# Latent attention: causal masks added by 64-row instead of 32-row matmuls, and a new order of units and of other work on TensorE

## The chip, the cores and the metric

The kernel runs on one core of a Trainium2 chip. The metric is device time in microseconds for one execution of the whole program, as a median of runs.

## What is computed

The reference is a "macaron" block over x of shape 8 x 512 x 128 (batch, tokens, channels): a local-attention transformer at half weight, a latent attention, and the same transformer again.

```python
x = x + 0.5 * _L0_ffn_ref(_layernorm(x), ...)
x = x + _L0_attn_ref(_layernorm(x), ...)
x = x + 0.5 * _L0_ffn_ref(_layernorm(x), ...)
```

The change touches the middle line alone:

```python
k_eff = (W_dq.T @ W_uq.T @ W_uk).reshape(nh, hs, n_kvl)
v_eff = jnp.transpose((W_uv.T @ W_o.T).reshape(n_kvl, nh, hs), (1, 0, 2))
c_kv = x @ W_dkv.T
q = (x @ W_dq.T @ W_uq.T).reshape(B, T, nh, hs)
q_lat = jnp.einsum('bqhd,hdl->bhql', q, k_eff)
attn = jnp.einsum('bhql,bkl->bhqk', q_lat, c_kv) / sqrt(hs)
attn = jnp.where(causal[None, None], attn, -jnp.inf)
attn = jax.nn.softmax(attn, axis=-1)
y_lat = jnp.einsum('bhqk,bkl->bhql', attn, c_kv)
y = jnp.einsum('bhql,hld->bqhd', y_lat, v_eff).reshape(B, T, C)
```

There are 16 heads of 8 channels, 512 tokens, and a causal mask.

## The kernel before

The program has three parts: the first transformer (`ffn("f0")`), `latent_attention`, and the second transformer (`ffn("f1")`). The two transformers are ordered by a planner with costs and places; the latent attention is ordered by hand, in the loop at the end of `latent_attention`, and `in_order` keeps every TensorE (PE) instruction in the order in which the program makes it.

**Layout.** The product of the weights is folded, so that a head's scores are a product over its 8 channels plus one more row. Heads lie in quadrants of 32 rows: head 4g + j has its channels in rows 32g to 32g + 8 of `q_heads` and `k_heads`, at index j. Row 32g + 8 (`MD::32`) holds the negated maximum on the query side and ones on the key side, so that the second pass over the scores comes out already shifted. Three sets of heads (`NSETS`) are used by turns over the 8 batches. A product over 32 rows occupies one quadrant of PE's rows (`32*128` in the profile), so that four can run side by side; the f32 products are made in two passes, which the trace shows as two matmuls with a weight load each. PSUM has seven banks of 512 columns for such products (`unit_bank`) and one for the values (`lo`).

**Two passes per batch.** `maxima_steps` (tile `sc`, lines L1038 and L1045) computes the scores with queries on partitions and reduces their maxima on DVE (L1051, L1053); its `finish` transposes them and sends them by a DMA into the heads. `sum_steps` (tile `st`, lines L1100 and L1107) computes the transposed scores, with keys on partitions; ACT takes the exponentials into `pl` (L1114). Both have ten steps a batch. A step has four units, one per quadrant g, and a unit fills one bank: one or two blocks of scores, 512 columns in all. The lists `MAXIMA` and `SUMS` say which blocks a unit holds; a unit has one or two blocks on the diagonal, which have to be masked.

**Masks.** The mask is added in PSUM by bf16 matmuls ahead of the f32 products: `rows_of` picks rows, and `causal` or `causal_t` holds the mask for them. A unit makes four such matmuls, each for 32 rows of the mask and in the unit's own quadrant (`quadrant(g)`). GpSimd (POOL) builds the three masks at the start of this part (L1205, L1213).

**Values.** `multiply` (L1123) multiplies the exponentials of a block by the values, for the four quadrants side by side in columns (`128*32`), into the bank `lo`; when a head group j has its four blocks, ACT copies the bank to `os` (L1132), and `update` transposes it (L1146), divides it by the sums (L1151, L1153) and adds it to X on POOL (L1157).

**The order.** Batch b's sums run beside the maxima of batch b + 1, which are two steps (`LEAD`) ahead. A step is made in two halves: `run_together([units[g], other[g]])` for g = 0 and 1, then for g = 2 and 3. `run_together` takes one matmul from each unit by turns. The maxima units are turned by two quadrants (`(g + 2) % 4`), so that the two units of a pair lie in different quadrants. Behind the first half come the products with the values of the step before (`held`). Behind the second half comes other work: a piece of the projections of batch b + 2 (`latent_project_steps`: normalisation, transposes, q, k, values, one piece a step from step 0 on), or a finished head group's `update`. The first batch's maxima run alone at the start; in the last two steps of the second-last batch and in the last batch there are no more maxima to run, and the sums run alone, two units at a time.

Of the kernel before, what the change touches and what calls it, by code (L numbers as in the profile page):

```python
# [9 lines left out]
BF16 = mybir.dt.bfloat16  # L10
AF = mybir.ActivationFunctionType
ALU = mybir.AluOpType
# [3 lines left out]
P = 128  # L16
MASKED = -1.0e30
# [172 lines left out]
def kernel(  # L190
# [22 lines left out]
    B, T, C = x.shape  # L213
# [17 lines left out]
    wk, lw, lp, lc = (PartPool() for _ in range(4))  # L231
# [88 lines left out]
    for first in (True, False):  # L320
        band = const.tile([P, 4, P], BF16, name=f"band{int(first)}")
        nc.gpsimd.memset(band, 0.0)
        for half in (0, WIN):
            rows = band[half : half + WIN]
# [14 lines left out]
    for l in range(L):  # L339
        t = const.tile([P, 4, NB, DH], F32, name=f"tab{l}")  # L340
        for s in range(2):
            g = qk_sc[:, l, s]
# [614 lines left out]
    def in_order(ins):  # L957
        return tc.keep_in_program_order(ins)
# [3 lines left out]
    def heads_of(b):  # L962
        return q_heads[b % NSETS], k_heads[b % NSETS], v_heads[b % NSETS]
# [49 lines left out]
    def quadrant(g):  # L1013
        return slice(32 * g, 32 * g + 32)


    MAXIMA = (
        [[((3, j), 0)] for j in range(4)]
# [4 lines left out]
    def maxima_steps(b):  # L1023


        qp, kp, _ = heads_of(b)
        nm = sm.tile([P, 4, 4, NB], F32, tag="lnm", name=f"lnm_{b}")

        nb = sm.tile([P, 4, 4, NB], F32, tag="lnb", name=f"lnb_{b}")

        def unit(held, g):
            rows = quadrant(g)
            (i0, j0), _ = held[0]
            bank = unit_bank(f"sc_{b}_{i0}_{j0}_{g}")
            blocks = bank.rearrange("p (n w) -> p n w", w=P)
            diag = {3: blocks[:, 3:], 2: blocks[:, 2:], 1: blocks[:, 1::2]}[i0]
            for k in range(4):
                yield lambda k=k: nc.tensor.matmul(  # L1038
                    diag[:, :, 32 * k :], lhsT=masks["rows_of"][rows, k],
                    rhs=masks["causal"][rows, k, 32 * k :].unsqueeze(1)  # L1040
                    .to_broadcast([32, len(held), P - 32 * k]),
                    start=(k == 0), stop=False, skip_group_check=True,
                )
            for n, ((i, j), at) in enumerate(held):
                yield lambda i=i, j=j, at=at, n=n: nc.tensor.matmul(  # L1045
                    bank[:, at : at + (i + 1) * P], lhsT=qp[rows, j, i * P : (i + 1) * P],
                    rhs=kp[rows, j, : (i + 1) * P],
                    start=False, stop=(n == len(held) - 1), skip_group_check=True,
                )
            if i0 == 2:  # L1050
                nc.vector.tensor_reduce(nb[:, g, j0], blocks, AX.X, ALU.max, negate=True)  # L1051
            else:
                nc.vector.tensor_reduce(  # L1053
                    nm[:, g, j0 : j0 + len(held), i0],
                    bank.rearrange("p (u w) -> p u w", u=len(held)), AX.X, ALU.max, negate=True,
                )

        def finish():
            nc.vector.tensor_reduce(nm[:, :, :, 2], nb[:, :, :, 0:3], AX.X, ALU.min)
            nc.vector.tensor_copy(nm[:, :, :, 0], nb[:, :, :, 3])  # L1060
            tp = unit_bank(f"tp_nm_{b}")
            in_order(nc.tensor.transpose(
                tp[: 16 * NB, :P], nm.rearrange("p g j n -> p (g j n)"), ident
            ))
            nT = lw.tile([16 * NB, P], F32, tag="lnT", name=f"lnT_{b}")
            nc.vector.tensor_copy(nT, tp[: 16 * NB, :P])
            nc.sync.dma_start(out=qp[MD::32], in_=nT)

        return [[unit(held, (g + 2) % 4) for g in range(4)] for held in MAXIMA], finish


# [13 lines left out]
    def sum_steps(b):  # L1085
# [5 lines left out]
        def unit(held, g, res):  # L1091
            rows = quadrant(g)
            (c0, j0), _ = held[0]
            bank = unit_bank(f"st_{b}_{j0}_{c0}_{g}")

            blocks = bank.rearrange("p (n w) -> p n w", w=P)
            diag = {0: blocks[:, :1], 1: blocks[:, ::3], 2: blocks[:, ::2]}[c0]
            for k in range(4):
                cut = 32 * k + 32
                yield lambda k=k, cut=cut: nc.tensor.matmul(  # L1100
                    diag[:, :, :cut], lhsT=masks["rows_of"][rows, k],
                    rhs=masks["causal_t"][rows, k, :cut].unsqueeze(1)
                    .to_broadcast([32, len(held), cut]),
                    start=(k == 0), stop=False, skip_group_check=True,
                )
            for n, ((c, j), at) in enumerate(held):
                yield lambda c=c, j=j, at=at, n=n: nc.tensor.matmul(  # L1107
                    bank[:, at : at + T - c * P],
                    lhsT=kp[rows, j, c * P : (c + 1) * P], rhs=qp[rows, j, c * P :],
                    start=False, stop=(n == len(held) - 1), skip_group_check=True,  # L1110
                )
            pr = lp.tile([P, 512], F32, tag="pl", name=f"pl_{b}_{j0}_{c0}_{g}")
            with exponentials():
                nc.scalar.activation(pr, bank, AF.Exp, scale=MSCALE)  # L1114
            res[g] = pr
# [19 lines left out]
        def values(held, res):  # L1135


            todo = kept + [(c, j, at, res) for (c, j), at in held if j == held[0][0][1]]
            kept[:] = [(c, j, at, res) for (c, j), at in held if j != held[0][0][1]]
            rest = [multiply(*what) for what in todo]  # L1140
            return next((r for r in rest if r is not None), None)

        def update(j, os_):
            tp = unit_bank(f"tp_o_{b}_{j}")
# [22 lines left out]

    def run_together(units):

        units = [u for u in units if u is not None]  # L1170
        while units:
            for u in list(units):
                ins = next(u, None)
                if ins is None:
                    units.remove(u)
                else:
                    in_order(ins())


    q_heads, k_heads, v_heads = [], [], []  # L1180
    masks = {}

    def latent_attention():
        no_shift = lc.tile([4, T], F32, tag="no_shift", name="no_shift")
# [16 lines left out]


        for name in ("rows_of", "causal", "causal_t"):
            masks[name] = lc.tile([P, 4, P], BF16, tag=name, name=name)
            nc.gpsimd.memset(masks[name], 0.0)  # L1205
        for g in range(4):
            for name, pattern, sign, op, fill in (
                ("rows_of", [[-32, 4], [1, P]], -1, ALU.not_equal, 1.0),
                ("causal", [[32, 4], [-1, P]], 1, ALU.is_ge, MASKED),
                ("causal_t", [[-32, 4], [1, P]], -1, ALU.is_ge, MASKED),  # L1210
            ):
                rows = masks[name][quadrant(g)]
                nc.gpsimd.affine_select(  # L1213
                    out=rows, in_=rows, pattern=pattern, compare_op=op, fill=fill, base=0,
                    channel_multiplier=sign,
                )
        for k in range(1, NSETS):
            blank(k, nc.gpsimd)
        full = latent_weights()
# [9 lines left out]
            maxima.append(steps)  # L1229
        assert len(maxima[0]) == NS  # L1230
        for step in maxima[0]:
            run_together(step[:2])
            run_together(step[2:])
        ahead = [step for steps in maxima[1:] for step in steps]
        after = []
        finish[0]()
        for _ in range(LEAD):
            step = ahead.pop(0)
            run_together(step[:2])
            run_together(step[2:])  # L1240
        held = None
        projecting = None
        for b in range(B):
            for s, (units, values) in enumerate(sum_steps(b)):
                other = ahead.pop(0) if ahead else None
                if s == 0 and b + 2 < B:
                    projecting = latent_project_steps(b + 2, full, no_shift)
                for half in (0, 2):
                    if other is not None:
                        for g in (half, half + 1):  # L1250
                            run_together([units[g], other[g]])
                    else:
                        run_together(units[half : half + 2])
                    if half == 0 and held is not None:
                        rest = held()
                        if rest is not None:
                            after.append(rest)
                held = values
                if s == NS - LEAD and b + 1 < B:
                    finish[b + 1]()  # L1260
                if projecting is not None and next(projecting, "end") == "end":
                    projecting = None
                if projecting is None and after:
                    after.pop(0)()
                elif len(after) > 1:
                    after.pop(0)()
        after.append(held())
        for rest in after:
            rest()

    with part(WORK_F, s=1, mm=1):
        ffn("f0", last=False)
# [89 lines left out]
```

## Time and profile before

| what | us |
|---|---|
| median of 3 runs (1949.81 to 1952.99) | 1952.13 |
| the profiled execution | 1953.01 |
| its span, first to last instruction | 1950.9 |
| from 792.8 to 829.8: the first batch's maxima and the two steps ahead | 37.0 |
| from 829.8 to 1153.2: sums and maxima side by side, 68 steps | 323.4 |
| from 1153.2 to 1200.5: sums alone, 12 steps | 47.3 |
| L1045 and L1107, f32 score products, 2 x 1024 matmuls (busy time) | 227.5 and 212.8 |
| L1114, exponentials, 320 of 597 ns (busy time) | 176.2 |

The profile is of one execution. Its groups give a line, an engine, an operation, the tiles and the shape with a count and a mean; `32*128` ahead of a shape is the part of PE's array, rows times columns, that a matmul uses. A matmul's start is recorded and its end is modelled; matmuls in different parts of the array overlap, so that busy times of groups add up to more than the stretch that they lie in. What a stretch costs is read from the distances of starts in the timeline. The granted TensorE clock is 0.984 of full speed as a mean.

### The profile page before, as it was taken

The numbers are of one execution on the slowest core, as the hardware profiler recorded it, in microseconds if no ns is written. First come the engines' busy times: TensorE is split into PE (matmuls) and PEld (weight loads), VectorE is DVE, ScalarE is ACT, GpSimd is POOL, SyncE is SP. The second block draws the span as 40 slices with busy tenths as digits, with TensorE's granted clock in tenths as the row PEclk, the third lists the DMA queues.
The fourth block names the chain that finished last, engine by engine and source line by source line (L and its number), as shares of the span: only waits on it lengthen the run. The fifth ranks groups of instructions, "written<-read, shape, count | busy, mean of one in ns | idle before, by whom it ended". The sixth has DMA issues, their size and how long they took to land.

```text
span 1950.9 us, 51021 instructions
## 1 busy us (share of the span) xinstructions
PE 1799.2 (92%) x19860; PEld 1186.0 (61%) x19860; DVE 1381.3 (71%) x2896; ACT 1394.7 (71%) x3921; POOL 985.4 (51%) x1673
## 2 busy tenths in 40 slices
PE   2889999999999997799999998889999999999998
PEld 1556666666666665566666663566666666666665
DVE  4888887777777775766655543887787777777764
ACT  1888888888888883155555554778888888888785
POOL 3876666666666653100000001867666666666651
PEclk9999999999999998799999998999999999999999
DMA  4111111111111110000000000111111011111110
GB/s 129 28 35 23 23 23 26 23 29 24 27 24 31 23 23 8 26 14 15 14 14 14 14 2 1 26 28 29 26 23 23 23 26 23 34 30 33 28 36 23
DMA packets 51729, 50.05 MB, mean 26 GB/s; under 512 B 23302, under 2 KB 34288, under 8 KB 51488
## 3 DMA queue, kind: packets, MB, share of 16 engines
q1 hardware_dynamic: 47132, 42.58, 9.3%
q10 hardware_dynamic: 4356, 4.20, 0.7%
q8 instruction: 158, 2.59, 0.6%
q14 instruction: 83, 0.68, 0.1%
HBM read 6.30 MB, written 2.10 MB: 4 GB/s over the span
## 4 chain that ended last, share of the span: by engine, by line
PE 56%; DVE 23%; ACT 11%; issue 5%; POOL 3%; DMA 1%; SPq 0%; ACTq 0%; DVEq 0%; POOLq 0%
PE mm_f L535 8%; PE mm_f L504 7%; PE mm_f L836 6%; ACT pr_f L679 5%; PE st L1107 5%; DVE c_f L545 5%; DVE s_f L548 4%; PE lo L1123 4%; PE mm_f L878 4%; PE sc L1045 4%; PE mm_f L745 4%; PE mm_f L769 4%; ACT sq_f L558 3%; PE sc_f L662 3%; PE st L1100 2%
## 5 line engine op out<-in xcount | busy, mean ns | idle before, releaser
L679 ACT ACTIVATE pr_f<-sc_f,nm_f,q_f 128x128 f32<-128x128 f32 x1024 | 460.2, 474 | 4.5 <-DVE nm_f L672 4.1
L535 PE MATMUL mm_f<-wqkv,hT_f 128*128 128x512 f32 x768 | 395.1, 616 | 35.7 <-DVE s_f L548 11.8
L564 POOL TENSOR_TENSOR qk_f<-c_f,s_f 128x512 f32<-128x512 f32 x256 | 324.5, 1271 | 109.8 <-DVE s_f L548 94.1
L687 POOL TENSOR_TENSOR pr_f<-pr_f,rso_f 128x512 f32<-128x512 f32 x256 | 265.8, 1039 | 215.2 <-DVE rso_f L703 142.1
L1114 ACT ACTIVATE pl<-st 128x512 f32<-128x512 f32 x320 | 176.2, 597 | 183.2 <-PE st L1107 111.8
L545 DVE TENSOR_TENSOR c_f<-mm_f,tab 128x512 f32<-128x512 f32 x256 | 175.2, 684 | 88.7 <-ACT sq_f L558 36.0
L558 ACT ACTIVATE sq_f<-mm_f 128x512 f32<-128x512 f32 x256 | 152.9, 603 | 115.1 <-DVE s_f L548 65.4
L1045 PE MATMUL sc<-k_heads,q_heads 32*128 32x384 f32 (+3 forms) x1024 | 227.5, 469 | 4.8 <-DMA k_heads<-kl 4.8
L679 ACT ACTIVATION_READ_ACCUMULATOR pr_f<-sc_f,nm_f,q_f 128x1 f32 x1024 | 225.1, 220 | 0.0
L1157 POOL TENSOR_TENSOR X<-X,lon 128x128 f32<-128x128 f32 x32 | 14.4, 452 | 402.6 <-DVE lon L1153 365.2
L1107 PE MATMUL st<-q_heads,k_heads 32*128 32x384 f32 (+3 forms) x1024 | 212.8, 435 | 0.0
L836 PE MATMUL mm_f<-fT_f,w 128*128 128x512 f32 (+1 forms) x384 | 189.9, 609 | 2.4 <-ACT fT_f L824 1.7
L504 PEld LDWEIGHTS mm_f<-ident,qk_f 128*128 128x128 f32 x1024 | 114.4, 142 | 125.1 <-POOL qk_f L600 50.2
L535 PEld LDWEIGHTS mm_f<-wqkv,hT_f 128*128 128x128 f32 x768 | 124.2, 192 | 100.8 <-issue 50.9
L745 PEld LDWEIGHTS mm_f<-pT_f,V_f 128*64 128x64 f32 (+1 forms) x4096 | 147.4, 136 | 55.3 <-issue 14.9
L671 DVE TENSOR_REDUCE nm_f<-sc_f 128x8 f32<-128x1024 f32 x128 | 154.7, 1209 | 36.9 <-PE sc_f L662 36.5
L745 PE MATMUL mm_f<-pT_f,V_f 128*64 128x64 f32 (+1 forms) x4096 | 179.8, 230 | 0.9 <-ACT pT_f L725 0.9
L504 PE MATMUL mm_f<-ident,qk_f 128*128 128x128 f32 x1024 | 161.6, 282 | 20.1 <-ACT kT_f L630 5.8
L548 DVE TENSOR_TENSOR s_f<-mm_f,tab 128x512 f32<-128x512 f32 x256 | 173.7, 678 | 0.0
L1053 DVE TENSOR_REDUCE lnm<-sc 128x1 f32<-128x512 f32 (+1 forms) x192 | 122.2, 685 | 71.6 <-PE sc L1045 49.7
L504 PE MATMUL mm_f<-ident,pr_f 128*128 128x128 f32 x1024 | 153.1, 278 | 11.8 <-ACT kT_f L630 6.2
L504 PEld LDWEIGHTS mm_f<-ident,pr_f 128*128 128x128 f32 x1024 | 117.4, 141 | 66.7 <-issue 39.8
(145 smaller groups left out, 3715.1 us busy)
## 6 DMA issues: line engine op xcount, KB each, us to landing
V_f<-V_f SPq DMA_DIRECT2D x224, 128.0 KB
hs_f<-Y SPq DMA_DIRECT2D x32, 112.0 KB
X<-in_x_dram SPq DMA_DIRECT2D x8, 256.0 KB
q_heads<-ql SPq DMA_DIRECT2D x64, 32.0 KB
k_heads<-kl SPq DMA_DIRECT2D x64, 32.0 KB
out_dram<-hs_f SPq DMA_DIRECT2D x8, 256.0 KB
wqkv<-in_wqkv_dram ACTq DMA_DIRECT2D x2, 768.0 KB
w<-in_w_dram ACTq DMA_DIRECT2D x2, 341.0 KB
```

The costliest lines, as they stand in the source:

```text
L504: nc.tensor.transpose(dst[:, i * P : (i + 1) * P], src(i), ident)
L535: nc.tensor.matmul(ps.tile, lhsT=hT[:, i * P : (i + 1) * P], rhs=wqkv_sb[l][:, at * INNER : (at + 1) * INNER], start=True, stop=True,)
L545: nc.vector.tensor_mul(c1.tile, psv, tabs[l][:, 2 * s, i].unsqueeze(1).to_broadcast([P, H, DH]))
L548: nc.vector.tensor_mul(s1.tile.rearrange("p h (t d) -> p h t d", t=2), psv.rearrange("p h (t d) -> p h t d", t=2)[:, :, ::-1], tabs[l][:, ...
L558: lambda s=s, ps=ps: nc.scalar.activation(sq[:, s], ps.tile, AF.Square),
L564: lambda s=s, c1=c1, s1=s1: nc.gpsimd.tensor_add(qk[:, s].rearrange("p (h d) -> p h d", d=DH), c1.tile, s1.tile),
L679: nc.scalar.activation(pr[:, h], sv[:, h % 2, h // 2], AF.Exp, bias=nm[:, h % 2, h // 2 : h // 2 + 1], scale=q8[:, h : h + 1], accum_out=s ...
L687: nc.gpsimd.tensor_mul(pr[:, heads], pr[:, heads], inv[:, heads].unsqueeze(2).to_broadcast([P, H // 2, P]),)
L745: nc.tensor.matmul(o[r * DH : (r + 1) * DH, u * P + w * WIN : u * P + (w + 1) * WIN], lhsT=(V2, V)[w][keys, i, h * DH : (h + 1) * DH], rhs ...
L836: nc.tensor.matmul(ps[: hsz[c], :], lhsT=w1_sb[l][:, at + c * P : at + c * P + hsz[c]], rhs=fT.tile, start=True, stop=True,)
L1045: yield lambda i=i, j=j, at=at, n=n: nc.tensor.matmul(bank[:, at : at + (i + 1) * P], lhsT=qp[rows, j, i * P : (i + 1) * P], rhs=kp[rows, ...
L1107: yield lambda c=c, j=j, at=at, n=n: nc.tensor.matmul(bank[:, at : at + T - c * P], lhsT=kp[rows, j, c * P : (c + 1) * P], rhs=qp[rows, j, ...
```

## The change

Masks are added by two matmuls of 64 rows in place of four of 32, in the half of the rows in which the unit's quadrant lies (`half_of`). `rows_of`, `causal` and `causal_t` have two blocks in place of four, and six selections build them in place of twelve.

`run_together` takes up to three units by turns and the fourth one behind them. It is called with all four units of a half step (sums, maxima, sums, maxima), with the four units of a step of the first batch's maxima, and with the four units of a step where sums run alone; the products with the values then come behind all four.

`values` returns its products one by one. In steps without a projection, a finished update or lone sums, the last product is made behind the second half. The projection pieces come in steps 1, 2, 4 and 6 (the normalisation ahead of step 0), and updates in other steps, when one was waiting at the step's start.

```diff
+    def half_of(g):
+        return slice(64 * (g // 2), 64 * (g // 2) + 64)
...
-            for k in range(4):
+            for k in range(2):
                 yield lambda k=k: nc.tensor.matmul(
-                    diag[:, :, 32 * k :], lhsT=masks["rows_of"][rows, k],
-                    rhs=masks["causal"][rows, k, 32 * k :].unsqueeze(1)
-                    .to_broadcast([32, len(held), P - 32 * k]),
+                    diag[:, :, 64 * k :], lhsT=masks["rows_of"][half_of(g), k],
+                    rhs=masks["causal"][half_of(g), k, 64 * k :].unsqueeze(1)
+                    .to_broadcast([64, len(held), P - 64 * k]),
                     start=(k == 0), stop=False, skip_group_check=True,
                 )
...
-            for k in range(4):
-                cut = 32 * k + 32
+            for k in range(2):
+                cut = 64 * k + 64
                 yield lambda k=k, cut=cut: nc.tensor.matmul(
-                    diag[:, :, :cut], lhsT=masks["rows_of"][rows, k],
-                    rhs=masks["causal_t"][rows, k, :cut].unsqueeze(1)
-                    .to_broadcast([32, len(held), cut]),
+                    diag[:, :, :cut], lhsT=masks["rows_of"][half_of(g), k],
+                    rhs=masks["causal_t"][half_of(g), k, :cut].unsqueeze(1)
+                    .to_broadcast([64, len(held), cut]),
...
-            rest = [multiply(*what) for what in todo]
-            return next((r for r in rest if r is not None), None)
+            return [lambda what=what: multiply(*what) for what in todo]
...
     def run_together(units):
-        units = [u for u in units if u is not None]
-        while units:
-            for u in list(units):
-                ins = next(u, None)
-                if ins is None:
-                    units.remove(u)
-                else:
-                    in_order(ins())
+        for some in (units[:3], units[3:]):
+            some = list(some)
+            while some:
+                for u in list(some):
+                    ins = next(u, None)
+                    if ins is None:
+                        some.remove(u)
+                    else:
+                        in_order(ins())
...
-            masks[name] = lc.tile([P, 4, P], BF16, tag=name, name=name)
+            masks[name] = lc.tile([P, 2, P], BF16, tag=name, name=name)
             nc.gpsimd.memset(masks[name], 0.0)
-        for g in range(4):
+        for g in (0, 2):
             for name, pattern, sign, op, fill in (
-                ("rows_of", [[-32, 4], [1, P]], -1, ALU.not_equal, 1.0),
-                ("causal", [[32, 4], [-1, P]], 1, ALU.is_ge, MASKED),
-                ("causal_t", [[-32, 4], [1, P]], -1, ALU.is_ge, MASKED),
+                ("rows_of", [[-64, 2], [1, P]], -1, ALU.not_equal, 1.0),
+                ("causal", [[64, 2], [-1, P]], 1, ALU.is_ge, MASKED),
+                ("causal_t", [[-64, 2], [1, P]], -1, ALU.is_ge, MASKED),
             ):
-                rows = masks[name][quadrant(g)]
+                rows = masks[name][half_of(g)]
...
         for step in maxima[0]:
-            run_together(step[:2])
-            run_together(step[2:])
+            run_together(step)
...
+            other_work = {1: "project", 2: "project", 4: "project", 6: "project"}
             for s, (units, values) in enumerate(sum_steps(b)):
                 other = ahead.pop(0) if ahead else None
-                for half in (0, 2):
+                halves = (0, 2) if other is not None else (0,)
+                due = len(waiting)
+                rest = []
+                for half in halves:
                     if other is not None:
-                        for g in (half, half + 1):
-                            run_together([units[g], other[g]])
+                        run_together([
+                            u for g in (half, half + 1) for u in (units[g], other[g])
+                        ])
                     else:
-                        run_together(units[half : half + 2])
+                        run_together(units)
                     if half == 0 and held is not None:
-                        rest = held()
-                        if rest is not None:
-                            after.append(rest)
+                        products = held()
+                        busy = other_work.get(s) or due or other is None
+                        while products and (busy or len(products) > 1):
+                            if (r := products.pop(0)()) is not None:
+                                waiting.append(r)
+                        rest = products
                 held = values
+                for r in rest:
+                    if (r := r()) is not None:
+                        waiting.append(r)
                 if s == NS - LEAD and b + 1 < B:
                     finish[b + 1]()
-                if projecting is not None and next(projecting, "end") == "end":
-                    projecting = None
-                if projecting is None and after:
-                    after.pop(0)()
-                elif len(after) > 1:
-                    after.pop(0)()
+                if project is not None and other_work.get(s):
+                    next(project, None)
+                elif due:
+                    waiting.pop(0)()
```

## The prediction

> **What bounds the kernel now.** I read the whole first: busy shares, then the chain that ended last.
>
> ```profile
> PE 1799.2 (92%) x19860; PEld 1186.0 (61%) x19860; DVE 1381.3 (71%) x2896; ACT 1394.7 (71%) x3921; POOL 985.4 (51%) x1673
> PE 56%; DVE 23%; ACT 11%; issue 5%; POOL 3%; DMA 1%; SPq 0%; ACTq 0%; DVEq 0%; POOLq 0%
> ```
>
> The edit touches the middle part alone, so next came windows over its three stretches: the first batch's maxima alone, 68 steps in which sums and the next batch's maxima run side by side (the "paired" steps), and 12 steps of sums alone.
>
> ```profile
> 792.80:829.80 37.00, 29.25 (x344) 20.59 (x343) 27.31 (x48) 0.59 (x1) 0.00 (x0) 0.82 0.08 24
> 829.80:1153.20 323.40, 323.40 (x4989) 213.00 (x4988) 196.23 (x378) 178.69 (x324) 11.75 (x26) 1.00 0.05 13
> 1153.20:1200.50 47.30, 47.30 (x540) 22.56 (x533) 4.32 (x13) 29.17 (x55) 2.25 (x5) 1.00 0.01 2
> ```
>
> Columns: length, then busy time of PE, weight loads, DVE, ACT, POOL. In the paired steps PE is never idle, DVE is at 61% and ACT at 55%: PE alone sets the time there, 4.76 us a step. But "busy" counts a PE with one quadrant of rows at work like one with four. So the timeline of one half step (PE only) came next.
>
> ```profile
> 953.39 0.18 PE L1100 MATMUL st<-causal_t,rows_of 32*128 32x32 bf16 x1
> 953.39 0.28 PE L1038 MATMUL sc<-causal,rows_of 32*128 32x256 bf16 x1
> ...
> 953.55 0.64 PE L1107 MATMUL st<-q_heads,k_heads 32*128 32x512 f32 x1
> ...
> 953.68 0.18 PE L1100 MATMUL st<-causal_t,rows_of 32*128 32x32 bf16 x1
> ...
> 954.03 0.59 PE L1107 MATMUL st<-q_heads,k_heads 32*128 32x512 f32 x1
> ...
> 954.38 0.70 PE L1045 MATMUL sc<-k_heads,q_heads 32*128 32x384 f32 x5
> 955.01 0.66 PE L1146 MATMUL tp_o<-ident,os 128*128 128x128 f32 x4
> 955.60 0.20 PE L1100 MATMUL st<-causal_t,rows_of 32*128 32x64 bf16 x1
> ```
>
> Here two pairs of units run in four quadrants. The second pair starts 0.29 us behind the first (953.68), long before the first pair's second f32 pass (954.03): instructions in different rows pass one another. From the first mask to the next full-height work the half step takes 955.01 - 953.39 = 1.62 us: 0.29 of lag, 0.29 of masks, 0.95 of f32 products, 0.09 until the transposes start. Such half steps with other kinds of units measure 1.63, 1.54 (maxima unit with one masked block, sums unit with two) and 1.32 (both with one).
>
> **How long a change of tile shape takes.** The f32 passes of 128 columns follow each other by 0.11 us in one shape. Between shapes:
>
> ```profile
> 402.14 0.60 PE L504 MATMUL mm_f<-ident,pr_f 128*128 128x128 f32 x4
> 402.67 0.45 PE L745 MATMUL mm_f<-pT_f,V_f 128*64 128x64 f32 x8
> ```
>
> The four passes started at 402.14 are through at 402.14 + 4 x 0.11 = 402.57, the next shape begins at 402.67: 0.10 us of nothing. I went through all changes of shape on PE (128 to 64 columns, 128 to 32 rows, 64x64 to 128x128, and back): 0.09 to 0.10 us as a rule, where nothing else is waited for. Even a change of columns alone, on the same rows, costs it, so I take it for the new changes between 64 and 32 rows as well. No row shows the two on different rows, which is what the change makes; that is the first rival.
>
> The page "TensorEngine Tiling (Array Packing)", section "Tiling Modes" (key properties), of the Trainium skill speaks against this change: it says that going over to another tiling mode, not just to another tile, empties the array first. The rows above agree with it at 0.09 to 0.10 us each; by it the sum is the forecast below, without it the first rival.
>
> **The change, part by part.** Call a half step's units A (sums), B (maxima), C (sums), D (maxima, now behind). A and C lie in one half of the rows and B and D in the other.
>
> *Masks.* A unit had 4 bf16 matmuls of 32 rows, 32 to 128 columns a block; it gets 2 of 64 rows, 64 and 128 columns. By start distances, 128 columns take 0.055 us and 64 take 0.028: a unit with one masked block goes from 0.165 to 0.083-0.094, with two from 0.29 to 0.165-0.176. But each new one holds two quadrants, so A's and C's masks queue up: 0.18 for two units with one block, 0.34 with two.
>
> *Order.* D's masks need the rows in which B multiplies, so they start when B is done, and D's f32 products then run with three quadrants empty. This is the cost of the change: two f32 stretches in a row where there was one and a lag of 0.29.
>
> *f32 stretch.* 2 passes of 512 columns at 0.43. The first pass also waits for its weights: before, the load went out during the last mask and 0.05 to 0.09 was left over (953.55 to 954.03 is 0.48); behind a change of shape all of it, 0.11, is open. So 0.965 us.
>
> *A half step after* = masks of A and C + 0.095 + 0.965 + 0.095 + masks of D + 0.095 + 0.965 + 0.093:
>
> - B/D two blocks, A/C two: 0.342 + 0.176 of masks, 2.83; before 1.63; +1.20, 56 times
> - B/D two, A/C one: 0.178 + 0.176, 2.66; before 1.63; +1.03, 28 times
> - B/D one, A/C one: 0.178 + 0.094, 2.58; before 1.32; +1.26, 26 times
> - B/D one, A/C two: 0.342 + 0.094, 2.74; before 1.54; +1.20, 26 times
>
> The counts come from the lists of held blocks over 68 steps. Sum: 67.2 + 28.8 + 32.8 + 31.2 = +160.0 us. The same bookkeeping for the kernel before gives 211 in half steps, 67 in products, 16 in transposes of outputs, 22 in projections, 2 in the transposed maxima, 318 in all, against 323.4 measured; of the 5.4 of stalls I let half go, as DVE and ACT get more slack: -2.7.
>
> *Sums alone.* A step now makes its four units and then multiplies; before, the products waited for the second half's exponentials (lo blocks of 2.0 us where 1.0 is usual). After: 6 x 2.83 + 4 x 2.58 + 10.0 (products) + 2.5 (transposes) = 39.8, before 1157.06 to 1198.19 = 41.1: -1.3.
>
> *The first batch's maxima.* PE would need 4 x 2.58 + 6 x 2.83 = 27.3 us, DVE's reductions 40 x 0.685 = 27.4; it took 26.4 behind the heads' arrival. Now two equal chains hand over to each other: +2, bounds 0 and +5.
>
> *Building the masks.* POOL makes 12 selections of 0.63 and 3 memsets of 0.53; six selections of half the columns remain. 4.3 us less if a selection costs the same, 6.2 if half. It isn't hidden altogether:
>
> ```profile
> 773.86 0.63 POOL L1213 TENSOR_SCALAR_AFFINE_SELECT causal_t<-causal_t 32x512 bf16<-32x512 bf16 x1
> 774.56 1.80 POOL L1194 MEMSET q_heads<- 128x2048 f32 x1
> ```
>
> ```profile
> 774.53 1.98 DVE L398 TENSOR_SCALAR xn<-X,mv_lat,ir_lat 128x128 f32<-128x128 f32 x2
> 786.94 1.09 DVE L398 TENSOR_SCALAR xn<-X,mv_lat,ir_lat 128x128 f32<-128x128 f32 x4
> ```
>
> Normalisations take 0.27 each once POOL's memsets end (786), and up to 1.7 while they run; these lie on the chain to the first maxima. Memsets that end earlier free DVE earlier, but would then meet DVE's own memsets: -3, bounds 0 and -6.
>
> *Other work.* The same products, transposes and projections, moved: one product to the end of two steps of a batch, k and v spread at steps 4 and 6 rather than 3 and 4. The k heads are needed by the maxima from step 8, some 28 us later, and their eight DMAs on SP's queue take 4.5 us to issue and 2.3 to land, so nothing waits. Every half step empties the array anyway: 0, bounds -2 and +3.
>
> *Sum:* 160.0 - 2.7 - 1.3 + 2.0 - 3.0 = +155, on the profiled execution's 1953.0 us: 2108. That execution is 0.9 above the median; 2107.
>
> **Rivals.**
>
> *The shapes mix without emptying the array.* For: all shown changes share rows. Then A's masks lie beside B's, three extra changes (0.29) and part of the open loads go, and the half steps become 2.33 (D with two blocks) and 2.16: 84 x 0.70 + 26 x 0.84 + 26 x 0.62 = +97; less 3 where two half steps touch, 2.7 of stalls, 6.4 in the sums alone, 3 in the opening: +82, 2034.
>
> *The fourth runs along (the other side).* If D's masks can pass B's f32 products in the queue, all four multiply together: half steps of 1.50 (1.33 with single blocks), -12 in the paired steps, -12 in the sums alone, -3 in the opening: 1925. It decides as soon as D starts less than 0.3 behind B. For: 953.68 above shows passing. Against: only between different rows; within one quadrant every start is in program order, and D's masks hold B's quadrant.
>
> The page "TensorE: Matmul & The Clock Gate", Part 3, of the skill has matmuls start and end strictly in order. The row at 953.68 differs from that; by the page this rival falls away, and the forecast stays.
>
> *Banks.* Three units now ask for three of seven banks at once; if each half step waited for one more eviction, 0.6 us x 136 = +82 on top, 2190. Against: PE gets slower, DVE and ACT do not, and the bank asked for was filled a whole half step earlier.
>
> **How the numbers follow.** Forecast 68%, its own range 2085 to 2128 (weights' cover, opening). No emptying 20%. Fourth along 6%. Banks or more 6%. The range reaches down to the first rival: 2028 to 2128. Some 0.2% is what a measurement can tell from no change; only the third case is faster: 0.06, nothing lies near zero (0.01), slower 0.93.
>
> **What would show it.** The paired stretch some 480 us long instead of 323; in a half step D's first mask about 1.3 to 1.4 us behind A's, then its f32 passes alone for 0.97; about 0.095 between the last mask and the first f32 pass; about 640 mask matmuls each for sums and maxima; ACT and DVE near 40% there. Wrong if the lo products start less than 1.6 us after a half step's first mask; the first rival if B's f32 passes start while A's or C's masks still run.

## The result

The changed kernel takes 2168.8 us (median of 4, 2166.3 to 2169.4) against 1951.0 for the kernel before: a ratio of 1.1113, with a 95% interval of 1.1094 to 1.1133. It is 218 us slower; 155 were forecast, and the time lies outside the range of 2028 to 2128. One run of a later kernel, the one with the filled wait, took 2199.4 us at a mean granted clock of 0.943 and is left out of that kernel's time and ratio.

The page of its profile, busy shares, then the granted clock in 40 slices, then the chain that ended last:

```profile
PE 2019.2 (93%) x18580; PEld 1236.6 (57%) x18580; DVE 1394.3 (64%) x2896; ACT 1387.5 (64%) x3921; POOL 980.1 (45%) x1667
PEclk9999999999999965599999999999999999999999
PE 62%; DVE 19%; ACT 9%; issue 4%; POOL 3%; DMA 1%; SPq 0%; ACTq 0%; DVEq 0%; POOLq 0%
```

PE has 220 us more busy time and 1280 matmuls fewer. What stands out is the clock: three slices at 0.5 to 0.6, in the latent part, where the kernel before had one at 0.7. Windows over the latent part say where (length; busy time of PE, weight loads, DVE, ACT, POOL with counts; then the granted clock):

```profile
793.70:845.70 52.00, 49.59 (x202) 23.01 (x202) 26.07 (x42) 0.00 (x0) 0.00 (x0) 0.50 0.04 12
845.70:855.50 9.80, 9.77 (x35) 3.07 (x35) 4.75 (x8) 0.00 (x0) 0.00 (x0) 0.50 0.04 7
855.50:920.00 64.50, 64.50 (x278) 29.03 (x278) 16.66 (x33) 13.60 (x26) 0.00 (x0) 0.50 0.02 5
920.00:1372.80 452.80, 452.80 (x3631) 231.90 (x3628) 192.53 (x344) 163.96 (x300) 11.72 (x26) 0.98 0.03 8
1372.80:1420.60 47.80, 47.80 (x425) 22.19 (x421) 2.91 (x10) 27.39 (x53) 1.80 (x4) 1.00 0.01 2
```

From 793.7 to 920.0 us PE runs at half clock, although it is busy nearly all of the time. The granted clock is either 1.00 or 0.50 in these traces; I call what switches it the clock gate, open at 1.00 and shut at 0.50. By stages, from the starts in the trace:

| stage | before | after | forecast |
|---|---|---|---|
| first batch's maxima, from the heads' arrival | 26.4 | 50.4 | 28.4 |
| two steps ahead | 5.5 | 9.8 | 5.5 (not costed, so unchanged) |
| paired steps | 323.5 | 516.6 | 481 |
| sums alone | 47.0 | 49.3 | 45.7 |

Now a half step of the paired stage at full clock (two masked blocks in each unit):

```profile
1000.69 0.23 PE L1103 MATMUL st<-causal_t,rows_of 64*128 64x128 bf16 x1
1000.69 0.28 PE L1041 MATMUL sc<-causal,rows_of 64*128 64x256 bf16 x1
...
1001.12 0.59 PE L1110 MATMUL st<-q_heads,k_heads 32*128 32x384 f32 x1
1001.12 0.48 PE L1048 MATMUL sc<-k_heads,q_heads 32*128 32x256 f32 x1
...
1002.19 0.34 PE L1041 MATMUL sc<-causal,rows_of 64*128 64x256 bf16 x2
1002.46 1.13 PE L1048 MATMUL sc<-k_heads,q_heads 32*128 32x256 f32 x4
1003.51 0.71 PE L995 MATMUL pv<-full_wv,xT 128*128 128x128 f32 x4
```

Masks of three units, 0.43 with the change of shape; the first f32 stretch from 1001.12; the fourth unit's masks only at 1002.19, and its f32 passes alone from 1002.46. Maxima unit B, whose masks were through earlier, starts its f32 passes at 1001.12 with the sums units: the array empties as a whole. The half step takes 1003.51 - 1000.69 = 2.82 us; 2.83 was forecast. The other kinds measure 2.66, 2.58 and 2.74, as forecast. At full clock the changes from 64 to 32 rows (320 in all) show 0.091 to 0.094 us of nothing between the last stream's end and the next start, and those from 32 to 64 rows (182) 0.093 to 0.096; at half clock both take 0.134.

A half step of the same kind at half clock:

```profile
877.87 0.28 PE L1103 MATMUL st<-causal_t,rows_of 64*128 64x128 bf16 x1
...
878.62 0.79 PE L1110 MATMUL st<-q_heads,k_heads 32*128 32x256 f32 x1
...
880.63 0.50 PE L1041 MATMUL sc<-causal,rows_of 64*128 64x256 bf16 x2
881.06 2.07 PE L1048 MATMUL sc<-k_heads,q_heads 32*128 32x384 f32 x4
883.06 0.85 PE L1126 MATMUL lo<-pl,v_heads 128*32 128x384 f32 x2
```

5.19 us, 1.84 times as long. So every microsecond with the gate shut costs about 0.456 us (1 - 1/1.84).

### The profile page after: what moved, and what is told of

Read it like the earlier page. It is cut to its first block, busy times and chain, and to the rows that moved or that the text cites. A ratio compares the mean times of both kernels' runs of the same rounds, so it can differ in the third digit from the quotient of the medians.

```text
span 2167.2 us, 48442 instructions
## 1 busy us (share of the span) xinstructions
PE 2019.2 (93%) x18580; PEld 1236.6 (57%) x18580; DVE 1394.3 (64%) x2896; ACT 1387.5 (64%) x3921; POOL 980.1 (45%) x1667
## 4 chain that ended last, share of the span: by engine, by line
PE 62%; DVE 19%; ACT 9%; issue 4%; POOL 3%; DMA 1%; SPq 0%; ACTq 0%; DVEq 0%; POOLq 0%
PE sc L1048 10%; PE st L1110 8%; PE mm_f L535 7%; PE mm_f L504 7%; PE mm_f L836 6%; DVE c_f L545 4%; DVE s_f L548 4%; PE lo L1126 4%; ACT pr_f L679 4%; PE mm_f L878 4%; PE mm_f L745 3%; PE mm_f L769 3%; ACT sq_f L558 3%; PE st L1103 3%; PE sc_f L662 2%
## 5 line engine op out<-in xcount | busy, mean ns | idle before, releaser
L1048 PE MATMUL sc<-k_heads,q_heads 32*128 32x384 f32 (+3 forms) x1024 | 379.6, 534 | 6.2 <-DMA k_heads<-kl 6.2
L1056 DVE TENSOR_REDUCE lnm<-sc 128x1 f32<-128x512 f32 (+1 forms) x192 | 131.3, 691 | 194.6 <-PE st L1110 118.6
L1048 PEld LDWEIGHTS sc<-k_heads,q_heads 32*128 32x128 f32 x1024 | 171.0, 212 | 63.1 <-issue 27.4
L1110 PE MATMUL st<-q_heads,k_heads 32*128 32x384 f32 (+3 forms) x1024 | 194.2, 487 | 0.0
L1054 DVE TENSOR_REDUCE lnb<-sc 128x4 f32<-128x512 f32 x128 | 87.6, 690 | 143.0 <-PE sc L1048 91.0
```

Source lines behind the costliest of these rows:

```text
L1048: yield lambda i=i, j=j, at=at, n=n: nc.tensor.matmul(bank[:, at : at + (i + 1) * P], lhsT=qp[rows, j, i * P : (i + 1) * P], rhs=kp[rows, ...
L1110: yield lambda c=c, j=j, at=at, n=n: nc.tensor.matmul(bank[:, at : at + T - c * P], lhsT=kp[rows, j, c * P : (c + 1) * P], rhs=qp[rows, j, ...
```

## The experiments

The first four separate the parts of the change.

**All four by turns, 64-row masks.**

```diff
-        for some in (units[:3], units[3:]):
+        for some in (units,):
```

> The changed kernel with one edit: all four units of a half step take turns, none is left behind; the masks stay at 64 rows. Theory (the f32 products of the unit behind run with three quadrants empty; a change between 64 and 32 rows costs 0.095 us; with so few quadrants at work the clock gate closes): a half step is masks 0.18 or 0.34 + 0.095 + 0.965 + 0.093, so 1.33 to 1.50 us; the granted clock stays at 1.0 behind the opening; 1925 us, 1915 to 1945. Rival (the 64-row masks and their changes of shape are the cost in themselves, the order matters little): 2080 us or more.

1965.8 us, ratio 1.0074 (1.0050 to 1.0099), where 1925 was expected. With 64-row masks, the unit behind carries nearly all of the cost: the paired steps fall from 516.6 to 342.1. Half steps behind long work take 1.51 us (1.50 expected). Two things were missed: the gate stays shut until 845.7 here as well, and half steps behind a short piece take up to 2.25, since the fourth unit's bank isn't empty yet (shown in the fourth run).

**64-row masks alone, in the old pairs.**

```diff
-            for k in range(4):
+            for k in range(2):
...
-                    diag[:, :, 32 * k :], lhsT=masks["rows_of"][rows, k],
+                    diag[:, :, 64 * k :], lhsT=masks["rows_of"][half_of(g), k],
```

> The kernel before with one edit: the 64-row masks; its pairs stay as they are. Theory: the second pair's masks are of another shape than the first pair's f32 products, so the pairs no longer overlap and a half step is twice (masks 0.09 to 0.18 + 0.095 + 0.965 + 0.095), 2.5 to 2.7 us; 2100 us with the clock open, up to 2165 if two quadrants of four leave it shut as three and one do. Rival (64-row and 32-row work on different rows mix freely, the order alone is the cost): 1940 to 1960.

2147.4 us, ratio 1.1010 (1.0982 to 1.1038). Four rows of a half step:

```profile
1002.85 0.23 PE L1103 MATMUL st<-causal_t,rows_of 64*128 64x128 bf16 x1
...
1003.12 0.58 PE L1110 MATMUL st<-q_heads,k_heads 32*128 32x384 f32 x1
...
1004.18 0.23 PE L1103 MATMUL st<-causal_t,rows_of 64*128 64x128 bf16 x1
...
1005.50 0.42 PE L1126 MATMUL lo<-pl,v_heads 128*32 128x256 f32 x3
```

The second pair's masks begin 1.33 us behind the first's, where 32-row masks began 0.29 behind; two stretches one after the other, 2.65 us. In the old order too, 64-row masks behind other units' f32 products are enough for that. The gate was shut from 794.1 to 889.7 us here.

**32-row masks, all else as changed.** The two mask loops and the masks are those of before.

> The changed kernel with one edit: the masks of 32 rows, as before; the unit behind and the new order of other work stay. Theory: all work of a half step has one shape and the fourth unit has a quadrant for itself, so it starts some 0.3 us behind the first as the second pair did; paired half steps as before (1.3 to 1.65), the steps of sums alone 10 to 13 us shorter in all: 1939 us, 1930 to 1955. Rival (a unit behind costs its whole f32 stretch whatever the masks are): 2030 or more.

1940.2 us, ratio 0.9945 (0.9925 to 0.9965); 1939 was expected. Paired steps 323.0 us, sums alone 35.4 where it was 47.0. The unit behind is harmless as long as it needs only its own quadrant:

```profile
944.66 0.20 PE L1103 MATMUL st<-causal_t,rows_of 32*128 32x64 bf16 x1
...
944.97 0.45 PE L1041 MATMUL sc<-causal,rows_of 32*128 32x256 bf16 x4
...
946.29 0.41 PE L1126 MATMUL lo<-pl,v_heads 128*32 128x256 f32 x2
```

It starts 0.31 behind and the half step takes 1.63. So the order alone costs nothing (this run), and the 64-row masks cost little where all units take turns (the first run): what costs is a unit's 64-row masks behind other units' f32 products. Those masks differ from the products in shape and lie in rows where another unit multiplies; no run separates the two.

**Four by turns, 32-row masks.** Both edits together.

> The changed kernel with two edits: masks of 32 rows, and all four units by turns. Theory: no change of shape and no lag, a half step is masks 0.17 or 0.29 + 0.95 + 0.09, so 1.10 to 1.33 us; 36 us less in the paired steps and 13 less in the sums alone than before: 1904 us, 1895 to 1925. Rival (four banks asked for at once make PE wait for evictions): 1935 or more, with waits of PE on DVE or ACT in the paired steps.

1941.3 us, ratio 0.9946 (0.9925 to 0.9967): the rival of the banks holds in part. Half steps behind long work do take 1.33. Behind a short piece:

```profile
962.71 1.08 ACT L1117 ACTIVATE pl<-st 128x512 f32<-128x512 f32 x2 [0.61 <-PE st L1110]
...
963.30 0.20 PE L1103 MATMUL st<-causal_t,rows_of 32*128 32x64 bf16 x1
...
963.85 0.26 PE L1041 MATMUL sc<-causal,rows_of 32*128 32x256 bf16 x1 [0.26 <-ACT pl L1117]
```

The exponentials of the half step before end at 963.79; the fourth unit's first mask takes that bank at 963.85, and the other units' next masks, which come later in the program, stand behind it for 0.5 us. This order also kept the clock at 0.50 from 798.2 to 849.4.

**Why the clock stayed at half.** For each window of 3.41 us (the changes of the clock lie on multiples of it) I worked out a fill of the array from the trace: the streaming time of each matmul (0.43 us for 512 f32 columns, twice that at half clock) times its share of the rows and columns, over the window. In the runs so far:

| kernel | window from | fill | gate |
|---|---|---|---|
| before | 799.0 | 0.83 | opens |
| before | 805.8 to 816.1 | 0.45 to 0.47 | stays open |
| before | 819.5 | 0.20 | shuts |
| after | 906.3 (streaming 91% of the time) | 0.59 | stays shut |
| after | 909.7 | 0.72 | stays shut |
| after | 916.6 | 0.73 | opens |
| after | 1155.5 (streaming 80% of the time) | 0.35 | shuts |
| four by turns, 32 rows | 811.9 to 825.5 | 0.70 to 0.73 | stays shut |
| four by turns, 32 rows | 846.0 | 0.90 | opens |

The same working from 130 to 1900 us of all twelve traces of this document gives 6232 windows. The gate opened behind 74 of them, with fills of 0.72 or more, and stayed shut behind fills of up to 0.75. It shut behind 74, all with fills of 0.40 or less; of the windows behind which it stayed open, all but two (0.31 and 0.35) had 0.37 or more. The time in which anything streams doesn't decide it: the gate shut behind windows that streamed 0.82 of the time, and stayed open behind others that streamed 0.52 to 0.60. The next runs test that.

**Filling the wait ahead of the maxima.**

```diff
+        warm = unit_bank("warm")
+        for _ in range(9):
+            in_order(nc.tensor.matmul(
+                warm, lhsT=wqkv_sb[0][:, :P], rhs=wqkv_sb[0][:, :512], start=True, stop=True,
+            ))
         for step in maxima[0]:
```

> The changed kernel with nine more matmuls of 128x128 by 512 columns in f32 that nobody reads, made while PE waits for the heads' DMAs ahead of the first maxima (a wait of 8.5 us). Clock theory (the 61 us beyond the forecast are the 0.50 clock from 793.7 to 920.0 us, which opens only after a window of 3.4 us in which about 0.74 of the array was filled, and closes below about 0.38): the wait no longer shuts the gate; the first batch's maxima take 26 to 29 us instead of 50, the two steps ahead 5 instead of 10, the paired steps 480 to 487 instead of 517; half steps stay 2.58 to 2.83; 2108 us, 2100 to 2122. Rival (the unit behind itself shuts the gate, or the 61 us are stalls): 2150 or more.

2151.5 us, ratio 1.1028 (1.1003 to 1.1053): a miss; 2108 was expected. The wait wasn't what shut the gate:

```profile
797.50:804.80 7.30, 7.30 (x46) 2.57 (x42) 5.93 (x10) 0.00 (x0) 0.00 (x0) 1.00 0.19 56
804.80:841.70 36.90, 36.15 (x161) 18.92 (x160) 19.85 (x33) 0.00 (x0) 0.00 (x0) 0.50 0.00 0
```

It was open when the maxima began and shut at 804.8, after a window with a fill of 0.35, in the midst of busy PE. Worked out: a step of lone maxima with single blocks streams 0.85 of f32 in four quarters and four times 0.08 of masks in halves, 1.01 us of full array in 2.58, a fill of 0.39, at the edge. The rival's first half was right: the changed steps, with a unit behind, shut the gate themselves. The first 7.3 us at full clock shortened the first batch's maxima from 50.4 us to 44.2.

**The same matmuls 60 us later.** They stand behind the two steps ahead.

> The same nine matmuls, made only after the two steps ahead, when the gate has been shut for 62 us. Clock theory: the opening stays at 50 us and the steps ahead at 10; the matmuls cost 11 to 12 us and open the gate; the paired steps take 480 to 487; 2147 us, 2140 to 2158. Rival (as above): 2170 to 2180, the cost of the matmuls on top.

2172.4 us, ratio 1.1115 (1.1062 to 1.1169); the runs lie between 2152.5, the profiled one, and 2176.8, so the median shows no gain; 2147 was expected, and it lies where the rival was. In the profiled run the gate opened, shut again after a window at 0.36, and opened at 889.4, with one more dip of 10 us at 1288.8:

```profile
864.80:872.40 7.60, 7.60 (x53) 3.07 (x52) 3.46 (x5) 2.97 (x6) 0.00 (x0) 1.00 0.00 0
872.40:889.40 17.00, 17.00 (x84) 7.86 (x86) 5.60 (x17) 3.45 (x8) 0.00 (x0) 0.50 0.00 1
```

Its paired steps took 490.4. Where the gate stood in the other runs isn't known, but for their mean clock: 0.957 to 0.959, against 0.970.

**Four by turns, 32-row masks, with the filled wait.**

> All four units by turns with 32-row masks, and the nine matmuls in the wait for the heads. Clock theory: the 0.50 clock from 798 to 849 us goes; the opening takes 26 to 28 us instead of 32.6, the paired steps 312 instead of 318; 1929 us, 1922 to 1936. The half steps that begin behind a short piece still wait for the fourth unit's bank, so it stays above the 1904 expected for no such waits.

1939.9 us, ratio 0.9940 (0.9923 to 0.9958), no gain beyond noise over 1941.3; 1929 was expected. The gate shut at 805.4, after a window with a fill of 0.30. Here no unit comes behind: PE was busy for 1.88 of 3.40 us and waited for DVE's reductions to empty the banks, with DVE busy throughout.

```profile
802.00:805.40 3.40, 1.88 (x29) 0.84 (x32) 3.40 (x7) 0.00 (x0) 0.00 (x0) 1.00 0.21 61
```

**The fourth behind only after short pieces.**

```diff
+                        ], 3 if half == 0 and (s % 2 == 0 or s == 9) else 4)
```

> As the kernel with four by turns, 32-row masks and the nine matmuls, but in the first half of those steps that follow a short piece (transposes or one short product) the fourth unit comes behind. Bank theory (the fourth unit's mask waits for the exponential that empties its bank and, as PE takes its queue in order, holds up the other three by 0.5 us): these half steps take 1.6 us from their first mask instead of 1.85, some 40 of them: 8 to 10 us less than the kernel without it, 1920 us, 1912 to 1930. Rival (the unit behind costs as much as the wait): no difference within 3 us.

1935.8 us, ratio 0.9917 (0.9893 to 0.9941), 4 less than without, which is within the spread of the runs; 1920 was expected. Most of the half steps in question still take 1.85 to 2.12. In the one from 955.36 the exponentials of the half step before end at 955.85, and the fourth unit's first mask starts at 955.90, 0.54 behind the first instead of 0.31. In the one from 982.56 the third unit starts 0.21 behind as well, and the fourth 0.81. So the order moves the wait and doesn't remove it. The rival is nearer.

**The old opening with the changed steps.** The first batch's maxima and the two steps ahead use 32-row masks in pairs, with four unread f32 matmuls behind each of the first two paired steps.

> The changed kernel, but the first batch's maxima and the two steps ahead are made as before the change (32-row masks, in pairs), and four f32 matmuls of 512 columns that nobody reads stand behind each of the first two paired steps, whose fill is lowest (7 us in all). All other steps are the changed kernel's own. Clock theory (fill theory: the gate opens after a window of 3.4 us at a fill of 0.74 or more, shuts at 0.38 or less): the opening takes 26 to 27 us and the steps ahead 5, the gate is open from about 830, and the paired steps take 485 to 492, that is 475 at full clock, 7 for the extra matmuls and at most two dips of 10 us at half clock; 2117 us, 2108 to 2126. Rival (the unit behind costs more than its quadrants' time whatever the clock): paired steps of 510 or more, 2140 or more.

2128.7 us, ratio 1.0903 (1.0888 to 1.0918): 40 less than the changed kernel, 12 more than expected. The opening is that of before:

```profile
797.80:824.30 26.50, 23.53 (x281) 17.50 (x281) 24.29 (x42) 0.00 (x0) 0.00 (x0) 0.89 0.08 21
824.30:830.00 5.70, 5.70 (x51) 2.74 (x51) 3.27 (x6) 0.00 (x0) 0.00 (x0) 0.50 0.03 9
830.00:844.00 14.00, 14.00 (x39) 4.72 (x39) 4.64 (x8) 2.17 (x4) 0.00 (x0) 0.50 0.00 0
```

The gate opened at 844.0 and not at 830: the first two paired steps are too empty to open it (fills of 0.44 to 0.51), and it opened behind the window of the extra matmuls at 839.4 (1.00). That makes some 6 of the 12 us (0.456 x 14.0); the rest stays open. The paired steps took 501.0.

**What the shut gate costs in the paired steps.** Four kernels run the same paired steps under different clocks. Taking 0.456 of the shut time off:

| kernel | paired | shut time in it | less 0.456 of it |
|---|---|---|---|
| changed | 516.6 | 64.5 + 10.2 + 10.2 | 477.9 |
| wait filled | 504.9 | 38.7 + 10.2 + 10.2 | 477.9 |
| matmuls late | 490.4 | 17.0 + 10.2 | 478.0 |
| old opening, less 7.1 of extra matmuls | 493.9 | 14.0 + 10.2 + 10.2 | 478.2 |

At full clock the paired steps are 478 us, within 0.1%; forecast were 481. The first and the third row alone give the same price: 26.2 us for 57.7 us of shut gate, 0.454.

**The best of the parts.** The mixed order without extra matmuls, and the fourth behind in the opening.

> The mixed kernel (32-row masks, four units by turns behind long pieces, the fourth behind after short ones) without the extra matmuls, and with the fourth behind in the first batch's maxima and the two steps ahead. Fill theory: the opening has the clock of the kernel with 32-row masks and a unit behind (26.5 us, steps ahead 4.7), the paired steps 314 to 316; 1932 us, 1927 to 1937, faster than both kernels. Rival (four by turns shut the gate again later): 1938 or more.

1935.2 us, ratio 0.9916 (0.9903 to 0.9930): 16 us faster than the kernel before and 11% faster than the changed one. The opening took 26.6 as expected; but the gate, shut at 822.1 in the steps ahead, stayed shut until 839.2, 11.3 us into the paired steps, so that these took 318.7, not 315. That is the rival's mechanism, at a price of 5 us. 12 us of the gain are those of the new order in the sums alone.

## Why the prediction failed, step by step

**The bound and the unit behind: right.** PE sets the time, and the fourth unit starts when the others are through and multiplies alone. At full clock the four kinds of half steps came within 0.01 us of the forecast, and 478 us of paired steps stand against 481.

**The changes of shape: right.** 0.091 to 0.096 each at full clock, and B's f32 passes wait for A's and C's masks in other rows, so the first rival (shapes mix) is out. The run with pairs shows the same from another side. The sentence of the Trainium skill weighed there, page "TensorEngine Tiling (Array Packing)", section "Tiling Modes", that a change of mode empties the array, holds here for tiles on different rows as well.

**The fourth along: out.** It starts 1.34 to 1.50 us behind A's first mask at full clock. By turns it can run along; then the banks decide, which was the last rival's place. In the changed kernel itself the half steps leave no room for a wait on banks.

**Masks and sums alone: small.** The maxima's f32 products start 2.5 us earlier (-3 forecast). The sums alone took 2.3 more, where 1.3 less was forecast: the last batch alone came to 39.6 against 39.8, but the two lone steps before it, costed at nothing, took 8.2 where they had taken 3.9, since the paired steps no longer run into them. The part behind was 4.8 shorter; its cause stays open.

**The step that failed** is the one that isn't there: every duration came from rows at full clock, and the sum took it for granted that the clock would stay. The window of the opening before showed a clock of 0.82, and the prediction passed over it. The change lowers the fill of the array from four quadrants to three and then one; the gate shut in the wait ahead of the maxima, as it had before, but where it had then opened again after 6.8 us it now stayed shut for 126, and it shut twice more for 10. That is 38.7 us in the paired steps (0.456 x 84.9) and 26 in the opening and the steps ahead (60.2 against 33.9 forecast). With -3 in the paired steps, +4 in the sums alone and -5 behind, 155 becomes 216; the spans differ by 216.3. The paired steps' share is shown by four runs. The opening's is an estimate: no run made the changed opening at full clock throughout, but 0.456 of 60.2 would be 27. That the gate goes by the fill, and not by something that rises and falls with it, is worked out from the windows; no run changed the fill alone.

The page "TensorE: Matmul & The Clock Gate", Part 1, of the skill has the gate go by how busy PE was in windows of 3.4 us and warns of idle gaps. The window fits the trace; here the clock stayed at 0.50 from 855.5 to 920.0 with PE busy 64.50 of 64.50 us, so an idle gap isn't needed.

## What to carry to other kernels

Work side by side in quadrants needs neighbours of one tile shape. Here a matmul over two quadrants waited for the units in other rows, two changes of shape came with it at 0.09 us each, and whatever stood behind it in program order waited as well. Before a sum is trusted at today's clock, work out the fill of the array per 3.4 us after the change, not just whether PE is busy: in these traces the clock fell to half behind fills of 0.40 or less and came back only behind 0.72 or more, which the slower steps seldom reached by themselves. Four banks asked for at once want four emptied ones. With 32-row masks, a unit 0.3 us behind (1940.2 us) and four by turns that wait for a bank (1941.3 us) came to the same.

## What the hardware showed that I had not expected

The clock gate has memory: in the changed kernel's paired steps, fills of 0.38 to 0.63 held it open, while 0.36 to 0.72 didn't open it once it was shut. At half clock a half step takes 1.84 times as long, not 2. And matmuls of different quadrants start out of program order: in the kernel before, the second pair's masks start at 953.68 us, ahead of the first pair's second f32 pass at 954.03, which comes earlier in the program. The second pair starts 0.29 us behind the first with two masked blocks and 0.12 with one.
